# Turning every other slice of the second expert product in place, with GpSimd copying it channels-inside for the way back to the tokens

## The chip, the cores and the metric

The kernel runs on one core of a Trainium2 chip. A core has a matrix engine (TensorE, PE in the profile), three engines for elementwise work (VectorE or DVE, ScalarE or ACT, GpSimd or POOL), and queues that issue DMA transfers (SyncE or SP issues nearly all of them here). The engines run on their own and wait for each other through semaphores. The metric is the device time of one execution in microseconds (us); lower is better.

## The reference

An input of 8192 tokens with 512 channels goes through two layers, each followed by a sum with its own input and a layer norm. The first layer is a long convolution with gates; the change does not touch it. The second layer, cut to what matters:

```
grouped = x.reshape(B, g, t, d)                     # groups of t = 32 tokens
logits  = einsum("bgtd,des->bgtes", grouped, controller) + tie
perm    = logits == max(logits over the experts e)  # 0/1 choice, 32 experts x 4 sets
dispatched   = einsum("bgtd,bgtes->bgesd", grouped, perm)
inner        = relu(einsum("bgesd,desf->bgesf", dispatched, f1) + bias)
intermediate = einsum("bgesf,esfd->bgesd", inner, f2)      # the second expert product
out          = einsum("bgesd,bgtes->bgtd", intermediate, perm)   # back to the tokens
```

Everything is float32.

## The kernel before

`experts` takes the tokens in 4 blocks of 2048 (b.n = 0 to 3), each in two halves of 1024 tokens (u = 0, 1), which are 32 groups of 32 tokens. The 512 channels are taken in four slices of 128 (c = 0 to 3). For each block the steps are:

- `dispatch(b, k)` sums the tokens to the experts on PE (L863) and copies the result from PSUM (L874 on DVE, L876 on ACT).
- `inner(b, k, ...)` multiplies with f1 (PE, L896) and adds into `b.h` on DVE (L902, L910, L912).
- `outer(b, u, c, halves)` is the second expert product for one half and one slice. For each of two halves of the experts it does 64 small matmuls in 32x32 tiles of the array (L933, fed by DMAs of f2 at L925), and two ACT copies (L942) bring the result from PSUM into `stage`. In `stage` a partition is an (expert set, group) pair, and along the partition lie [128 channels][32 experts]. After the second half, two DVE transposes in blocks of 32 x 32 (L946), 64 channels each, bring `stage` to `turned`; now a partition is an (expert set, expert) pair and along it lie [128 channels][32 groups].
- `back(b, u, c, turned)` is the way back to the tokens: for each of the 32 groups one matmul (L962) with the choice `b.permT` as weights (128 x 32) and the 128 channels of that group, `turned[:, :, group]`, as the streamed operand. Four groups go side by side to four column groups of the array. In the profile every f32 matmul is two instructions, so there are 64 per slice. DVE adds the result to `x1` (L969).
- `front(ahead, u)` does the same tokens' first steps for the next block in small pieces that are strewn between the others: A0 to A7 are the output projection of the first layer (`project`: DMA of xt at L750, GpSimd's add of the bias at L772, PE L774, DVE L779), N0 to N3 the norm and its turn (L800, L805, L807), C0 and C1 the choice (L817, L822, L827, L828), T0 and T1 its turn (L836, L837).
- `finish(b, u)` is the last layer norm of a half (L1069 to L1090, with the small chain L721 to L727 and L1077 on DVE and the scaling L1084 on ACT).

`stage` and `turned` are the two halves of one tile:

```
b.big = wk.tile([P, 2, P, T], F32, tag="big", name=f"si_{b.n}_{u}_{c}")
stage, turned = b.big[:, 0], b.big[:, 1]
```

The tag "big" has two buffers, which `dispatch` uses too. PSUM tiles of all these steps come from one pool of four pairs of banks.

The order of PE's work is the order of the program (a manual schedule); for the other engines a scheduler places the instructions. In the loop over slices the way back of a slice is done only after the product of the next slice:

```
outer(b, u, c, [0]); fa(amid)
turned = outer(b, u, c, [1]); fb(behind)
if last: back(*last)
last = (b, u, c, turned)
```

where `fa` and `fb` are pieces of `front` for the next block. The last slice of a block, (u, c) = (1, 3), is sent back between the first two parts and the last two parts of the next block's first `dispatch`. This loop runs for blocks 0, 1 and 2. The last block has an order of its own (`last_block`), with its own product, its transposes in place (L1042) and the same `back_on_pe`.

Of the kernel before, what the change touches and what calls it, by code (L numbers as in the profile page):

```python
# [18 lines left out]
P = 128  # L19
# [4 lines left out]
T = E  # L24
# [655 lines left out]
def experts(tc, i, load, y_dram, out):  # L680
# [10 lines left out]
    nc = tc.nc  # L691
    with (
# [20 lines left out]
        def pair(name):  # L713
            return pp2.tile([P, 1024], F32, tag="pp", name=name)
# [199 lines left out]
        def outer(b, u, c, halves):  # L914


            if halves[0] == 0:
                b.big = wk.tile([P, 2, P, T], F32, tag="big", name=f"si_{b.n}_{u}_{c}")
            stage, turned = b.big[:, 0], b.big[:, 1]
            for half in halves:  # L920
                pss = [pair(f"pi_{b.n}_{u}_{c}_{half}_{rr}") for rr in range(2)]
                for two in range(2):
                    at = 4 * half + 2 * two
                    f2 = wk.tile([P, 2, S, P], F32, tag="f", name=f"f2_{b.n}_{u}_{c}_{at}", bufs=6)
                    nc.sync.dma_start(  # L925
                        out=f2.rearrange("p q s d -> p (q s d)"), in_=i["f2"][c, at // 2]
                    )
                    for q in range(2):
                        for s in range(S):
                            for r in range(R):  # L930
                                rows = slice(r * F, (r + 1) * F)
                                col = r % 2 * 512 + (2 * two + q) * P
                                nc.tensor.matmul(  # L933
                                    pss[r // 2][s * T : (s + 1) * T, col : col + P],
                                    b.h[rows, at + q, s, u * T : (u + 1) * T], f2[rows, q, s, :],
                                    start=True, stop=True,
                                )
                for rr in range(2):
                    o = stage.rearrange("p d (r q) -> p r d q", r=R)[
                        :, 2 * rr : 2 * rr + 2, :, 4 * half : 4 * half + 4  # L940
                    ]
                    nc.scalar.copy(o, pss[rr].rearrange("p (r q d) -> p r d q", r=2, q=4))  # L942
            if 1 in halves:
                for dh in range(2):
                    d = slice(dh * 64, (dh + 1) * 64)
                    nc.vector.transpose(  # L946
                        turned[:, d].rearrange("p d g -> p (d g)"),
                        stage[:, d].rearrange("p d e -> p (d e)"),
                    )
            return turned  # L950

        def back(b, u, c, turned):
# [150 lines left out]
        for n in range(NBLK):  # L1103
            b = Block()
# [4 lines left out]
        b = blocks[0]  # L1109
# [18 lines left out]
        for b in blocks:  # L1128
# [26 lines left out]
            for u in range(2 if ahead else 0):  # L1155
                for c in range(NCT):
                    fa, amid, fb, behind = slots[u * NCT + c]
                    outer(b, u, c, [0])
                    some(ends, 1)
                    fa(amid)  # L1160
                    turned = outer(b, u, c, [1])
                    some(ends, 1)
                    fb(behind)
                    if last:
                        back(*last)
                    if u == 1 and c == 0:
                        ends = finish(b, 0)
                    some(ends, 1)
                    last = (b, u, c, turned)
# [80 lines left out]
```

## Time and profile before

| what | value |
|---|---|
| time, median of 3 runs | 2242.71 us (2237.34 to 2244.29) |
| the profiled execution: its time | 2235.14 us |
| the profiled execution: its span, first to last instruction | 2233.3 us |
| PE clock granted, mean | 0.974 of full |
| the stretch 1576 to 1694 us (loop over slices of block 0): PE busy | 108.2 of 118 us |
| the same stretch: DVE, ACT, POOL busy | 78.0, 47.9, 10.0 us |
| L962, way back of the 24 slices of blocks 0 to 2: PE busy | 90.1 us (1536 instructions) |
| L946, the 48 transposes: DVE busy | 108.1 us |
| L772, GpSimd's adds: POOL busy | 60.6 us (48 instructions) |

The table is read like this: busy times are unions of the engine's instructions, so that matmuls running side by side count once. The loops over slices lie at 1576 to 1694 us (block 0), 1768 to 1890 us (block 1) and 1960 to 2083 us (block 2). In the profile `si` is the tile of `stage` and `turned`, `pc` the PSUM of the way back, `pi` that of the second product, `pd` that of `dispatch`, `xt` the input rows with bias. "PEld" is PE's weight load. A form like "128*32 128x128" names the rows and columns of the array that are used, and the size of the result.

### The profile page before, as it was taken

What the parts mean: (1) busy time and instruction counts of PE and PEld (TensorE: products, weight loads), DVE (VectorE), ACT (ScalarE), POOL (GpSimd) and SP (SyncE); (2) the same over time, 40 slices, a digit from 0 to 9 for tenths busy, and PEclk for the clock granted to TensorE, in tenths of its full rate; (3) what the DMA queues carried; (4) which work ended last, traced back from release to release, by engine and by line L of the source; (5) the groups of instructions that cost most, each with busy time, mean ns of one, the idle gap of its engine ahead of it and who ended that gap; (6) DMA issues with size and microseconds to landing.
All of it is one profiled execution on the core that took longest, in us unless ns stands there. A gap on an engine that the chain in (4) does not pass through costs nothing.

```text
span 2233.3 us, 65558 instructions
## 1 busy us (share of the span) xinstructions
PE 2073.7 (93%) x29472; PEld 1441.0 (65%) x29472; DVE 1380.7 (62%) x1864; ACT 795.7 (36%) x1272; POOL 676.9 (30%) x598
## 2 busy tenths in 40 slices
PE   8999999999998999999999999989999999999874
PEld 3343344444447999999999998555556556556653
DVE  6786776766765553463373373556676667766766
ACT  2444446555552321321221231021243235224424
POOL 3645747766750430250070071211100100110000
PEclk9999999999999999999999999999999999999897
DMA  5312312532434745664573565725763864665474
GB/s 153 105 40 74 104 48 76 198 132 76 145 129 122 220 152 203 194 211 171 161 256 134 180 210 189 241 72 160 235 205 110 270 200 158 207 230 182 135 245 163
DMA packets 187685, 362.60 MB, mean 162 GB/s; under 512 B 77911, under 2 KB 101341, under 8 KB 184333
## 3 DMA queue, kind: packets, MB, share of 16 engines
q1 hardware_dynamic: 181900, 340.05, 46.6%
q10 hardware_dynamic: 5504, 18.35, 2.2%
q8 instruction: 232, 3.80, 0.7%
q14 instruction: 49, 0.39, 0.1%
HBM read 274.47 MB, written 83.89 MB: 160 GB/s over the span
## 4 chain that ended last, share of the span: by engine, by line
PE 73%; DVE 14%; ACT 7%; issue 3%; DMA 2%; POOL 1%; ACTq 0%; DVEq 0%; SPq 0%; POOLq 0%
PE p L329 15%; PE px L588 10%; PE pa L564 10%; PE po L774 10%; PE pz L621 5%; PE py L649 5%; PE pc L962 4%; PE pi L933 3%; PE ph L896 3%; PE pd L863 3%; PE pl L817 2%; ACT o L391 2%; PE pk L286 1%; DVE pf L256 1%; DVE o L407 1%
## 5 line engine op out<-in xcount | busy, mean ns | idle before, releaser
L329 PE MATMUL p<-xs,win 128*128 128x512 f32 x768 | 354.7, 606 | 13.5 <-POOL xs L208 11.2
L329 PEld LDWEIGHTS p<-xs,win 128*128 128x128 f32 x768 | 145.1, 193 | 196.5 <-issue 170.8
L329 PE MATMUL p<-xq,win 128*128 128x512 f32 x576 | 258.7, 597 | 7.4 <-DMA win<-in_W_in 5.3
L610 POOL TENSOR_TENSOR place<-t,hs 128x256 f32<-128x256 f32 x132 | 94.8, 718 | 480.2 <-DVE hs L608 410.2
L774 PE MATMUL po<-wout,yt 128*128 128x512 f32 x512 | 238.1, 611 | 2.3 <-issue 1.9
L564 PE MATMUL pa<-c_in_sb,vk 128*64 128x128 f32 x4096 | 227.3, 274 | 8.1 <-DVE w L414 5.4
L564 PEld LDWEIGHTS pa<-c_in_sb,vk 128*64 128x64 f32 x4096 | 225.7, 138 | 9.9 <-issue 9.5
L588 PE MATMUL px<-place,tab 128*64 128x128 f32 x4096 | 228.1, 273 | 1.7 <-ACT place L571 1.6
L588 PEld LDWEIGHTS px<-place,tab 128*64 128x64 f32 x4096 | 226.1, 136 | 3.1 <-ACT place L571 2.6
L329 PEld LDWEIGHTS p<-xq,win 128*128 128x128 f32 x576 | 109.5, 191 | 147.9 <-issue 134.0
L772 POOL TENSOR_TENSOR xt<-xt,bout 128x512 f32<-128x512 f32 x48 | 60.6, 1285 | 460.3 <-DMA xt<-in_x 385.6
L774 PEld LDWEIGHTS po<-wout,yt 128*128 128x128 f32 x512 | 94.9, 194 | 110.9 <-issue 103.9
L573 DVE COPY place<-pa 128x1024 f32<-128x1024 f32 x64 | 78.3, 1225 | 139.9 <-PE pa L564 136.1
L425 POOL TENSOR_TENSOR w<-o,w 128x512 f32<-128x512 f32 x92 | 114.5, 1274 | 162.6 <-ACT w L397 107.4
L942 ACT COPY si<-pi 128x1024 f32<-128x1024 f32 x96 | 92.9, 1015 | 190.1 <-PE pi L933 156.8
L571 ACT COPY place<-pa 128x1024 f32<-128x1024 f32 x64 | 64.8, 1012 | 254.8 <-PE pa L564 246.8
L407 DVE SCALAR_TENSOR_TENSOR o<-u,chan_sb,o 128x512 f32<-128x512 f32 x192 | 136.4, 746 | 29.4 <-ACT o L391 28.8
L946 DVE STREAM_TRANSPOSE si<-si 128x2048 f32<-128x2048 f32 x48 | 108.1, 2291 | 59.4 <-ACT si L942 59.4
L391 ACT ACTIVATE o<-u,bias,chan_sb 128x512 f32<-128x512 f32 x192 | 141.0, 767 | 0.0
L621 PE MATMUL pz<-c_back_sb,place 64*128 64x128 f32 x2048 | 122.7, 282 | 14.5 <-POOL place L610 14.5
L621 PEld LDWEIGHTS pz<-c_back_sb,place 64*128 64x128 f32 x2048 | 121.9, 198 | 15.4 <-POOL place L610 15.4
L603 ACT COPY hs<-px 128x512 f32<-128x512 f32 x132 | 75.6, 573 | 156.6 <-PE px L588 151.1
(114 smaller groups left out, 3155.5 us busy)
## 6 DMA issues: line engine op xcount, KB each, us to landing
f<-in_f SPq DMA_DIRECT2D x160, 512.0 KB, 5.4
tab<-in_c_mid SPq DMA_DIRECT2D x64, 512.0 KB, 3.8
place<-in_c_out SPq DMA_DIRECT2D x64, 512.0 KB, 4.7
gate<-w SPq DMA_DIRECT2D x32, 512.0 KB, 4.1
x<-w SPq DMA_DIRECT2D x32, 512.0 KB, 3.0
taps<-taps SPq DMA_DIRECT2D x4, 4096.0 KB, 11.1
vk<-taps SPq DMA_DIRECT2D x32, 512.0 KB, 4.0
vk<-gate SPq DMA_DIRECT2D x32, 512.0 KB, 3.7
```

Of the source, the lines that this page charges most:

```text
L329: nc.tensor.matmul(ps, win[self.m][:, slot, self.s, k, :], self.x[tokens][:, k, :], start=(k == 0), stop=(k == 1),)
L391: nc.scalar.activation(pss[n], u[:, t0 + 2 : t0 + 2 + TB], AF.Identity, bias=bias[:, at : at + 1], scale=ch[:, at, 4:5],)
L407: nc.vector.scalar_tensor_tensor(o, u[:, t0 + 1 : t0 + 1 + TB], ch[:, at, 3:4], ps, ALU.mult, ALU.add)
L425: nc.gpsimd.tensor_tensor(wn, o, wn, ALU.add)
L564: nc.tensor.matmul(ps[r * 64 : (r + 1) * 64, c * N1 : (c + 1) * N1], vk[:, half * 8 + c, :], cin[:, r, :], start=True, stop=True,)
L588: nc.tensor.matmul(ps[h * 64 : (h + 1) * 64, j, :, r, :], tab[:, g % 2 * KC + j, r * 64 : (r + 1) * 64], both[:, :, g * KC + j, h * 64 : ( ...
L610: nc.gpsimd.tensor_tensor(o[:, 0], t[:, 0], hs[:, 1], ALU.subtract)
L621: nc.tensor.matmul(ps[:, h, c, :], spec[rows, r, c0 + c, :], cback[rows, r].rearrange("p q n -> p (q n)"), start=(r == 0), stop=(r == 1),)
L649: nc.tensor.matmul(ps[:, q, :], z[:, r * N2 + n0 + q, :], tab[:, q % 4, r, :], start=(r == 0), stop=(r == 1),)
L774: nc.tensor.matmul(ps, got["y"][:, ct, t % 2 * P : (t % 2 + 1) * P], wout[:, ct, :], start=(ct == 0), stop=(ct == NCT - 1),)
L942: nc.scalar.copy(o, pss[rr].rearrange("p (r q d) -> p r d q", r=2, q=4))
L946: nc.vector.transpose(turned[:, d].rearrange("p d g -> p (d g)"), stage[:, d].rearrange("p d e -> p (d e)"),)
```

## The change

For slices with odd c, `turned` gets another layout: along the partition lie [32 groups][128 channels] instead of [128 channels][32 groups], in the same memory. The two DVE transposes of such a slice write back over `stage` instead of into `turned`, and after each of them two GpSimd copies bring its 64 channels to `turned`, 16 groups at a time; they read one element every 32 and write runs of 64 channels. The way back then reads the 128 channels of a group side by side. Slices with even c are as before. It concerns 12 of the 24 slices of blocks 0, 1 and 2; the last block is unchanged.

```diff
@@ outer
             stage, turned = b.big[:, 0], b.big[:, 1]
+            if c % 2:
+                turned = turned.rearrange("p a b -> p (a b)").rearrange("p (g d) -> p d g", d=P)
             for half in halves:
...
             if 1 in halves:
                 for dh in range(2):
                     d = slice(dh * 64, (dh + 1) * 64)
-                    nc.vector.transpose(
-                        turned[:, d].rearrange("p d g -> p (d g)"),
-                        stage[:, d].rearrange("p d e -> p (d e)"),
-                    )
+                    half = stage[:, d].rearrange("p d e -> p (d e)")
+                    if c % 2 == 0:
+                        nc.vector.transpose(turned[:, d].rearrange("p d g -> p (d g)"), half)
+                        continue
+                    nc.vector.transpose(half, half)
+                    for g0 in range(0, T, 16):
+                        nc.gpsimd.tensor_copy(
+                            turned[:, d, g0 : g0 + 16].rearrange("p d g -> p g d"),
+                            stage[:, d, g0 : g0 + 16].rearrange("p d g -> p g d"),
+                        )
             return turned
```

## The prediction

> **What bounds the kernel now.** First the page, its busy times and its chain of work that ended last:
>
> ```profile
> PE 2073.7 (93%) x29472; PEld 1441.0 (65%) x29472; DVE 1380.7 (62%) x1864; ACT 795.7 (36%) x1272; POOL 676.9 (30%) x598
> ...
> PE 73%; DVE 14%; ACT 7%; issue 3%; DMA 2%; POOL 1%; ACTq 0%; DVEq 0%; SPq 0%; POOLq 0%
> ```
>
> PE sets the end. The edit pays where it shortens PE's own work, and costs where PE must wait. It touches `outer`, which runs for 3 blocks x 2 halves x 4 slices = 24 slices; 12 of them have odd c. I write c1, c3 for the odd slices of half 0 and (1,1), (1,3) for those of half 1.
>
> Second, the way back to the tokens (L962) beside two other matmul lines, from the views by source line (ns: min/median/max):
>
> ```profile
> L962 PE MATMUL pc<-si,permT x1536: 377/395/400, 1598.7 to 2079.0; 128*32 128x128 f32 x192
> ...
> L863 PE MATMUL pd<-perm,x x2048: 269/270/578, 1481.0 to 2119.2; 32*128 32x128 f32 x187
> L896 PE MATMUL ph<-dT,f x4096: 216/219/315, 1512.0 to 2138.1; 128*32 128x64 f32 x196
> ```
>
> L863 and L962 both stream 128 columns of f32, but L962 takes 125 ns more. L863 reads its columns side by side; L962 reads `turned[:, :, g]`, a column every 32 elements. L896 has L962's weight shape (128*32), reads 64 columns side by side and shows no such excess: 51 ns under L863 for 64 columns fewer, 0.8 ns a column. So the excess goes with the stride.
>
> Third, the timeline of PE, DVE and POOL around c1 of block 0 and, further down, half 1 (start, duration):
>
> ```profile
> 1596.26 4.51 DVE L946 STREAM_TRANSPOSE si<-si 128x2048 f32<-128x2048 f32 x2 [1.74 <-ACT si L942]
> 1596.91 2.52 POOL L772 TENSOR_TENSOR xt<-xt,bout 128x512 f32<-128x512 f32 x2 [17.32 <-DMA xt<-in_x]
> ...
> 1613.27 3.68 PE L962 MATMUL pc<-si,permT 128*32 128x128 f32 x64
> ...
> 1649.51 2.50 POOL L772 TENSOR_TENSOR xt<-xt,bout 128x512 f32<-128x512 f32 x2 [26.05 <-DMA xt<-in_x]
> 1649.82 0.98 DVE L724 TENSOR_TENSOR rt<-rs 128x4 f32<-128x4 f32 x1
> 1650.84 1.19 DVE L725 TENSOR_TENSOR rt<-rt,ve 128x4 f32<-128x4 f32 x1
> ```
>
> The first pair of transposes is c1's; its way back starts only 12.5 us after they end, because PE does the next slice first. That gap is where the copies must fit. The last three lines show DVE and POOL in each other's way: L724 usually takes 0.16 us and here ends with the first POOL add (1650.76), L725 with the second. The transposes at 1596.26 overlapped POOL adds and kept their 2.25 us each, so transposes are not held.
>
> Fourth, what POOL's instructions cost (groups by shape, POOL alone):
>
> ```profile
> L757 POOL TENSOR_TENSOR xt<-xt,bout 128x1024 f32<-128x1024 f32 x8 | 19.5, 2443 | 96.0 <-DMA xt<-in_x 80.5 <-DMA yt<-y 15.5
> masks.py:199 POOL TENSOR_SCALAR_AFFINE_SELECT ident<-ident 128x128 f32<-128x128 f32 x1 | 0.3, 294 | 0.1
> masks.py:197 POOL MEMSET ident<- 128x128 f32 x1 | 0.2, 205 | 6.7 <-DMA y<-place 6.7
> ```
>
> **The change part by part.**
>
> *Shorter way back on 12 slices.* Now 64 instructions take 3.68 us: 57.5 ns each, and with four column groups side by side 230 ns for 128 columns, 1.80 ns a column. L896, same weight shape and columns side by side, issues 128 in 1.99 us: 15.5 ns, four groups 62 ns for 64 columns, 0.97 ns a column. At that pace the odd slices need 16 x 128 x 0.97 = 1.99 us, so 1.7 us less each: 12 x 1.7 = 20.3 us. Bounds: none if the stride is not the cause; 1.96 us each (23.5 us) if all of the streaming excess (125 of about 233 ns) goes.
>
> *Transposes in place.* 24 DVE instructions change only where they write. L1042 already does the same in place at 2277 ns against L946's 2291: nothing.
>
> *Copies.* 4 per odd slice, 48 in all, 128x1024 f32 each, reading a column every 32 elements and writing runs of 64. No copy by POOL stands in the trace. Low end: MEMSET's slope over the 0.10 us of a one-element memset, 0.105/128 = 0.82 ns an element, so 0.95 us. High end: the two-input add of the same size, 2.44 us, and for the stride that once more by the factor that PE loses to it (1.72 against 0.84 ns a column of streaming, 2.05): 5.0 us. The nearest form is the affine select, one input and one output: (294 - 100)/128 = 1.5 ns an element, 1.65 us a copy. I take 1.65, 6.6 us a slice.
>
> [...]
>
> *Do they fit?* The first copy may start when the first transpose ends, and POOL must have done the xt add queued ahead. From there to L962's start, blocks 0/1/2: c1 13.8/12.2/12.9 us (POOL's L772 of A6 ends last, at 1599.43 in block 0), c3 13.6 in all, (1,1) 10.6/9.9/10.7, (1,3) 7.9/7.1/7.7. At 6.6 us all fit, (1,3) of block 1 with 0.5 us to spare; the limit there is 1.78 us a copy. If that cover is gone, PE waits in order and all later matmuls with it, every microsecond in full.
>
> *What queues behind the copies.* On POOL the order is A6's adds, c1, next block's A0 adds, c3, A2's adds, (1,1), (1,3), A4's adds; in blocks 1 and 2 nearly the same. The adds behind (1,3) wait for their DMA until 1715.74, far after the copies: nothing. The adds ahead of c3 and (1,1) end at 1623.47 and 1652.01, before the copies could start: nothing. The order on PE, DVE, ACT and SP's queue is unchanged, and no DMA is moved.
>
> *DVE held by the copies.* Only instructions like L724 suffer. Around c1 and c3 that is one choice (L828) near the end of the copies: hidden. At (1,1) the copies run 1657.0 to 1663.6 and the small chain L721 to L1077 of `finish` starts at 1663.28: 0.3 us. Also at (1,1), L969 can't end earlier than now (transposes until 1670.68, then L822), which keeps some 0.3 us of the way back's gain. Together 0.6 us a block, 1.8 in all.
>
> Sum: -20.3 + 1.8 = -18.5 us. The profiled execution took 2235.14 us (span 2233.3), the median of the runs is 2242.71, 7.6 above it; the stage is the same in both, so I take the sum off the median: 2224 us.
>
> **The rivals.**
>
> *Copies at the rate of the two-input add, 2.44 us.* 9.8 us a slice: c1 and c3 fit (-1.7 each). At (1,3), gap 7.6 on average, PE waits 2.2 us: +0.5 net. At (1,1) they just fit, but hold DVE's small chain until 1667 or so: L1077 comes 3 us late, the next transposes 1.9 us late, L969 ends near 1674.5 and the matmul that needs its PSUM, at 1674.11 now, comes 0.4 us later than now with the gain gone: +0.4. Per block -2.5, in all -7.5: 2235. For it: stride, and all POOL rows of this size lie at 2.4 us. Against: those read two inputs.
>
> *Slower: the way back waits for GpSimd.* If the stride costs POOL its factor 2.05 on the 1.65 us, a copy takes 3.4 us, a slice 13.6. Late: c1 0.6, (1,1) 3.2, (1,3) 6.0, together 9.8 against a gain of 6.8 a block: +9 in all, 2252; at the ceiling of 5.0 us, late 35.4 a block, +86. It decides from about 3.1 us a copy: two gaps, (4x - 10.4) + (4x - 7.6) = 6.8. For it: the gap of (1,3) is the shortest, and nothing there hides PE. Against: POOL's own rows are far below.
>
> *The change doesn't do what it says for PE.* The 395 ns come from the way four column groups share the array, not from the stride; then the gain is nothing and copies of 1.65 us cost 0 to 2 us: 2243. With 2.44 us it would be +7 from (1,3) alone. Against: L896 has the same groups.
>
> **How the numbers follow.** Forecast 0.49 (-14 to -22 us over 1 to 2 us a copy). Two-input rate 0.22 (0 to -13, half beyond the bound). Late copies 0.18. No gain on PE 0.11 (half within the bound, half slower). A measurement here tells about 0.3%, 6.7 us, from no change. Faster 0.49 + 0.11 = 0.60; same 0.11 + 0.05 + 0.01 = 0.17; slower 0.17 + 0.06 = 0.23. The range goes from the larger saving, with the runs' own spread, 2215, to the first end of the late case, 2253; the forecast's own part of it is 2215 to 2230.
>
> **What would show it.** Right: L962 in two forms, half near 270 ns and 2.0 us a slice; POOL's copies at 1.0 to 1.8 us; no wait of PE on POOL; PE busy 20 us less. Wrong: PE idle before L962 released by POOL, at (1,3) first, then (1,1); L724, L725, L1077 stretched inside the copies; or L962 unchanged at 395 ns. A copy over 3.1 us would by itself make the change a loss.

## The result, and the profile after

The changed kernel takes 2234.34 us (median of 22 runs, 2226.65 to 2241.61) and the kernel before, run beside it, 2238.47 us (22 runs, 2232.96 to 2244.55). The ratio is 0.9975, 95% interval 0.9964 to 0.9986, which at 2238 us is -5.6 us (-8.1 to -3.1). The prediction was -18.5 us: the direction is right, the size is three times too large. The profiled execution took 2228.4 us (span 2226.6, 6.7 less than before; granted clock 0.971).

The page of the profile after, its busy times, chain and copies (group by line: count | busy, mean ns | idle before):

```profile
PE 2058.2 (92%) x29472; PEld 1437.6 (65%) x29472; DVE 1384.0 (62%) x1864; ACT 795.4 (36%) x1272; POOL 771.2 (35%) x646
...
PE 72%; DVE 16%; ACT 7%; issue 3%; DMA 2%; POOL 1%; ACTq 0%; DVEq 0%; POOLq 0%
...
L954 POOL COPY si<-si 128x1024 f32<-128x1024 f32 x48 | 93.3, 1995 | 99.8 <-DVE si L952 99.8
```

The changed line by source line (ns: min/median/max), the copies behind it:

```profile
L970 PE MATMUL pc<-si,permT x1536: 272/338/422, 1600.0 to 2074.3; 128*32 128x128 f32 x192
L954 POOL COPY si<-si x48: 1940/1987/2087, 1599.9 to 2069.8; 128x1024 f32<-128x1024 f32 x48
```

The timeline of block 0, the first odd slice and the copies of (1,1):

```profile
1597.08 2.50 POOL L772 TENSOR_TENSOR xt<-xt,bout 128x512 f32<-128x512 f32 x2 [16.37 <-DMA xt<-in_x]
1599.93 7.77 POOL L954 COPY si<-si 128x1024 f32<-128x1024 f32 x4 [0.35 <-DVE si L952]
...
1614.57 1.95 PE L970 MATMUL pc<-si,permT 128*32 128x128 f32 x64
...
1658.01 7.76 POOL L954 COPY si<-si 128x1024 f32<-128x1024 f32 x4 [2.57 <-DVE si L952]
```

The copies of c1 end at 1607.70, 6.9 us before its way back begins. The matmul of the way back is L970 now (L962 before); half of its instructions stand at 272 ns. A slice with channels inside takes 1.95 us where it took 3.68. Groups by shape, the three loops alone (1570 to 2090 us); in before L962 had 90.1 us there:

```profile
L970 PE MATMUL pc<-si,permT 128*32 128x128 f32 x1536 | 69.7, 335 | 4.2 <-issue 4.2
L721 DVE TENSOR_SCALAR ve<-mv 128x8 f32<-128x8 f32 x5 | 5.3, 1067 | 0.1
```

So the way back lost 20.4 us of PE's time, but PE as a whole lost 15.5 and the span 6.7. The views by line and the page's busy times account for it: -20.4 on the way back, +6.3 on four other matmul lines that run longer over the execution with nothing in them changed (L935 98.9 to 100.7, L863 85.3 to 88.0, L896 68.5 to 69.5, L817 59.3 to 60.1), -1.4 on the rest, and +8.8 of idle time. The rest has one unchanged line that runs shorter, the last block's product (31.8 to 28.5 us), so between two single executions such shifts go both ways.

The idle time, PE's waits in 1570 to 2090 us (us in total, times, longest). Before:

```profile
PE pi L933 <- issue: 11.3, 13, 2.7
PE pi L933 <- ACT si L942: 3.8, 6, 0.8
```

After:

```profile
PE pi L935 <- issue: 14.5, 15, 2.5
PE pi L935 <- ACT si L944: 7.9, 6, 2.1
PE pc L970 <- issue: 4.2, 4, 2.2
PE ph L896 <- issue: 3.6, 2, 2.7
PE pxT L805 <- DVE permT L822: 2.7, 2, 1.6
```

All "issue" waits in this window together rose from 15.8 to 23.0 us, the wait of the second product for ACT by 4.1 us, and a wait of N-turns for L822 is new. The first of these is not like for like: the work stands some 5 us earlier after the change, and the same wait falls behind the window before and into it after:

```profile
2094.56 0.32 PE L896 MATMUL ph<-dT,f 128*32 128x64 f32 x7 [2.92 <-issue]
```

```profile
2089.95 0.49 PE L896 MATMUL ph<-dT,f 128*32 128x64 f32 x13 [2.66 <-issue]
```

Over the same instructions the "issue" waits are 18.7 us before and 23.0 after; the change run again (e15 below) has 20.4. For POOL PE waited only once, 0.36 us at (1,3) of block 0, where the way back took 2.31 us instead of 1.95.

The longer lines come with a lower clock. Windows of the loops (width, busy of PE, PEld, DVE, ACT, POOL; then PEclk), first before, then after:

```profile
1570.00:2090.00 520.00, 488.09 (x11924) 306.61 (x11926) 353.42 (x503) 191.00 (x227) 45.26 (x36) 0.99 0.58 192
```

```profile
1570.00:2090.00 520.00, 475.13 (x12029) 304.36 (x12031) 361.38 (x510) 190.97 (x227) 139.12 (x85) 0.97 0.60 195
...
1714.70:1718.10 3.40, 1.30 (x34) 1.03 (x32) 3.30 (x8) 1.97 (x2) 2.45 (x2) 1.00 0.64 259
1718.20:1724.90 6.70, 6.02 (x66) 4.63 (x67) 3.37 (x3) 2.02 (x2) 0.00 (x0) 0.50 0.01 2
1725.00:1728.00 3.00, 3.00 (x31) 1.28 (x32) 0.22 (x1) 0.00 (x0) 0.00 (x0) 1.00 0.00 0
```

PE worked 1.30 of 3.4 us, and the next 6.7 us ran at half clock. From 1570 us to the half-clock window behind the wait at L896 shown above (it ends at 2098.4 us before and at 2093.6 after), the trace has 17.1 us at half clock before (4 stretches) and 34.1 us after (8 stretches). The next stretch, 10.2 us, stands in both, at 2101.8 us before and at 2097.0 after.

### The profile page after: what moved, and what is told of

Same layout as the page of the kernel before. It is cut to its first block, busy times and chain, and to the rows that moved or that the text cites. A ratio compares the mean times of both kernels' runs of the same rounds, so it can differ in the third digit from the quotient of the medians.

```text
span 2226.6 us, 65625 instructions
## 1 busy us (share of the span) xinstructions
PE 2058.2 (92%) x29472; PEld 1437.6 (65%) x29472; DVE 1384.0 (62%) x1864; ACT 795.4 (36%) x1272; POOL 771.2 (35%) x646
## 4 chain that ended last, share of the span: by engine, by line
PE 72%; DVE 16%; ACT 7%; issue 3%; DMA 2%; POOL 1%; ACTq 0%; DVEq 0%; POOLq 0%
PE p L329 15%; PE px L588 10%; PE pa L564 10%; PE po L774 9%; PE pz L621 6%; PE py L649 5%; PE pi L935 3%; PE ph L896 3%; PE pd L863 3%; PE pc L970 3%; PE pl L817 2%; ACT o L391 2%; PE pk L286 2%; DVE pf L256 1%; DVE o L407 1%
## 5 line engine op out<-in xcount | busy, mean ns | idle before, releaser
L944 ACT COPY si<-pi 128x1024 f32<-128x1024 f32 x96 | 93.0, 1014 | 180.5 <-PE pi L935 161.7
L621 PE MATMUL pz<-c_back_sb,place 64*128 64x128 f32 x2048 | 123.2, 283 | 14.5 <-POOL place L610 14.5
L954 POOL COPY si<-si 128x1024 f32<-128x1024 f32 x48 | 93.3, 1995 | 99.8 <-DVE si L952 99.8
```

Source lines behind the costliest of these rows:

```text
L621: nc.tensor.matmul(ps[:, h, c, :], spec[rows, r, c0 + c, :], cback[rows, r].rearrange("p q n -> p (q n)"), start=(r == 0), stop=(r == 1),)
L954: nc.gpsimd.tensor_copy(turned[:, d, g0 : g0 + 16].rearrange("p d g -> p g d"), stage[:, d, g0 : g0 + 16].rearrange("p d g -> p g d"),)
```

## The experiments

Ratios are to the kernel before, run beside it on the same chip; "us" is (ratio - 1) x 2238. Diffs are against the changed kernel.

| run | edit | ratio (95%) | us |
|---|---|---|---|
| the change | | 0.9975 (0.9964 to 0.9986) | -5.6 |
| e15_again | the change again | 0.9969 (0.9948 to 0.9990) | -6.9 |
| e1_nocopy | no copies | 0.9938 (0.9918 to 0.9959) | -13.9 |
| e2_copyonly | copies, way back as before | 0.9991 (0.9974 to 1.0009) | -2.0 |
| e3_direct | DVE writes the layout itself | 1.0074 (1.0053 to 1.0096) | +16.6 |
| e4_direct_all | the same, 24 slices | 1.0167 (1.0142 to 1.0192) | +37.4 |
| e5_shift | 64 more PE instructions ahead | 0.9968 (0.9948 to 0.9987) | -7.2 |
| e6_no11 | no copies at (1,1) | 0.9976 (0.9961 to 0.9991) | -5.4 |
| e7_small | copies in quarters | 0.9997 (0.9979 to 1.0015) | -0.7 |
| e8_later | last norm a slice later | 0.9977 (0.9960 to 0.9995) | -5.1 |
| e9_no_half1 | no copies in half 1 | 0.9949 (0.9929 to 0.9969) | -11.4 |
| e10_no_half0 | no copies in half 0 | 0.9949 (0.9925 to 0.9972) | -11.4 |
| e11_swap | odd slices of half 0, even of half 1 | 0.9993 (0.9976 to 1.0010) | -1.6 |
| e12_nocopy_all | no copies, 24 slices | 0.9894 (0.9869 to 0.9919) | -23.7 |
| e13_unawaited | copies that nobody awaits | 0.9955 (0.9937 to 0.9973) | -10.1 |
| e14_pick | c1, c3, (1,2), (1,3) | 0.9990 (0.9972 to 1.0008) | -2.2 |
| e16_cover | A7 moved over the wait | 0.9991 (0.9973 to 1.0009) | -2.0 |
| e17_cover_before | the same in before | 1.0009 (0.9995 to 1.0023) | +2.0 |
| e18_cover_nocopy | the same without copies | 0.9960 (0.9941 to 0.9980) | -9.0 |

**The two sides of the change alone.**

```diff
                     nc.vector.transpose(half, half)
-                    for g0 in range(0, T, 16):
-                        nc.gpsimd.tensor_copy(...)
+            if c % 2:
+                return stage.rearrange("p a b -> p (a b)").rearrange("p (g d) -> p d g", d=P)
             return turned
```

> The odd slices are transposed in place and the way back reads that same half of the tile as if the channels lay inside; the 48 copies by GpSimd are left out, so the odd slices carry wrong elements. PE keeps its shorter way back (1.95 us instead of 3.68), GpSimd does nothing there. Theory A (PE's saving of 20.4 us is paid out only in part, because other chains follow close behind: PE's own code supply, the gaps with releaser 'issue', and the DVE and ACT chain at the start of half 1): still only -7 to -12 us against the kernel before, because taking the copies away gives back at most the DVE instruction L721 that waits for GpSimd (1.5 us a block) and 0.4 us at (1,3). Theory B (the copies cost the missing 13 us, by holding DVE or by being late): -18 to -21 us.

```diff
-            return turned
+            return stage if c % 2 else turned
```

> The odd slices are transposed in place and GpSimd makes its 48 copies, but nobody reads them: the way back reads the transposed half with its stride, as before. The result is the reference's. Theory A: +0 to +4 us against the kernel before (the hold on DVE's L721 at (1,1), nothing else). Theory B: +10 to +14 us.

Measured: -13.9 us without copies (-18.4 to -9.2), -2.0 us with copies alone (-5.8 to +2.0). The first lies between the ranges of the two theories; the second is below both, with 0 inside its interval. So the copies cost nothing that shows beside the old way back, a faster way back without copies brings two thirds of its 20.4 us, and with both only a third is left. Something of PE's saving is lost even with no copy in the program. In the profile of e1 PE's idle time over the execution is 167.5 us (span less busy) against 159.6 before, and three waits of the second product show where it goes:

```profile
PE pi L935 <- issue: 15.6, 16, 3.7
PE pi L935 <- ACT si L944: 7.9, 6, 2.1
PE pi L935 <- DVE x L974: 3.7, 3, 1.7
```

Before, the same three are 11.3, 3.8 and 0.9 us.

**The layout without GpSimd.**

```diff
-                    nc.vector.transpose(half, half)
-                    for g0 in range(0, T, 16):
-                        nc.gpsimd.tensor_copy(...)
+                    nc.vector.transpose(turned[:, d], stage[:, d])
```

> The odd slices' transposes write the layout with the channels inside themselves (output pattern of 64 channels x 32 groups, a step of 128 between groups), no copies and no GpSimd. If a strided write costs DVE nothing (2.29 us stays), this is e1 with right results: theory A -7 to -12 us, theory B -18 to -21 us. If DVE pays for the stride as PE does for its read (double, 4.6 us a transpose, 55 us more DVE in the three blocks), PE waits for DVE at half 1 and the time is that of before or above, 0 to +15 us.

> As e3, for all 24 slices: PE has about 41 us less to do than before. Theory A: the gains stay partial, since the even slices' savings run into the same chains (code supply above all, which PE now outruns twice as often): -10 to -20 us against the kernel before. Theory B: -36 to -41 us, if transposes stay at 2.29 us. If they double, slower than before by 10 to 50 us.

 (the same edit for every c)

Both lose, by 16.6 and 37.4 us. Groups of e3 in 1570 to 2090 us, and two of its waits of PE there:

```profile
L952 DVE STREAM_TRANSPOSE si<-si 128x2048 f32<-128x2048 f32 x22 | 84.0, 3893 | 27.2 <-ACT si L944 27.2
L950 DVE STREAM_TRANSPOSE si<-si 128x2048 f32<-128x2048 f32 x24 | 54.1, 2291 | 34.2 <-ACT si L944 34.2
```

```profile
PE pi L935 <- DVE x L972: 11.1, 3, 3.9
PE pp L836 <- DVE x L972: 10.0, 3, 3.3
```

A transpose that writes with the step takes 3893 ns instead of 2291, and PE waits for DVE's add behind it. GpSimd was the cheaper place for the step here (-5.6 us with its copies, +16.6 us with DVE's step).

**Where PE waits with no releaser.** Counted over PE's records (weight loads, matmuls and its semaphore steps), the waits with no releaser between 1570 and 2090 us stand at one place of a group of 256: 18 of over 0.15 us (15.7 us) before, 22 (23.0 us) after. The page has the instruction queue (packets, MB, share of the DMA engines):

```profile
q8 instruction: 232, 3.80, 0.7%
```

That is 16.4 KB a packet, and 59389 records of PE over 256 make 232. The second product is 128 weight loads and 128 matmuls in 1.9 us, a whole group; where PE waited, the next group came 3.4 to 5.5 us after PE had entered the one before (8 in 10 of these 40 waits). In the kernel before, of the groups with at least 4.5 us of PE's work none of 60 ended in a wait, of those under it 18 of 34. e5 moves the code by 64 instructions, with 32 more turns in block 0:

```diff
-                    for k in range(NCT):
+                    for k in range(NCT * (5 if b.n == 0 and u == 0 and m == 0 else 1)):
+                        k = k % NCT
```

> The changed kernel with the 8 turns of the first norm (block 0, half 0, N0) done five times over: 32 turns more, 64 more PE instructions (weight load and matmul), same result, some 4 us more PE work at that place. Everything after it is the same code, 64 instructions later in PE's code. Theory A1 (PE's idle gaps that the trace calls 'issue' are PE waiting for its next 256 instructions, one of the 232 packets of 16 KB of queue q8): every such gap falls 32 weight load + matmul pairs earlier in the work. The gap of the changed kernel in the product after c1's way back, after 100 of 128 matmuls, stands after about 68; the one that is always there in c1's product after 126 stands after about 94; the sum of the gaps in the three blocks may change by some us either way, so the time is +0 to +8 us against the changed kernel (-6 to +3 against before). Theory A2 (the gaps are a wait for f2's data or for PSUM): they stay after 100 and 126 matmuls.

The product at 1591 us in block 0, after the change and in e5:

```profile
1591.71 1.89 PE L935 MATMUL pi<-f,h 32*32 32x128 f32 x126
1596.08 0.40 PE L935 MATMUL pi<-f,h 32*32 32x128 f32 x2 [2.48 <-issue]
```

```profile
1591.62 1.47 PE L936 MATMUL pi<-f,h 32*32 32x128 f32 x94 [0.61 <-DVE x L779]
1593.41 0.69 PE L936 MATMUL pi<-f,h 32*32 32x128 f32 x34 [0.32 <-issue]
...
1675.47 0.69 PE L936 MATMUL pi<-f,h 32*32 32x128 f32 x18 [3.09 <-issue]
```

The gap moved from after 126 matmuls to after 94, the 32 that went in: these waits are for code. c1's way back is 1.73 us shorter in both, but only in e5 does the stretch from c1's to c2's way back fall by as much (13.07 before, 12.43 after, 11.35 in e5, mean of the blocks); in the changed kernel code gaps eat most of the rest (0.33 and 0.83 us in block 0, 1.26 in block 1, 0.23 in block 2). e5 pays elsewhere (3.09 us at 1675), and its time is that of the change.

**The start of half 1.** c3's way back comes earlier, but DVE does not. PE's wait before, and the timeline after:

```profile
1649.71 0.88 PE L933 MATMUL pi<-f,h 32*32 32x128 f32 x42 [0.76 <-ACT si L942]
```

```profile
1641.55 4.50 DVE L950 STREAM_TRANSPOSE si<-si 128x2048 f32<-128x2048 f32 x2 [1.62 <-ACT si L944]
1643.14 1.95 PE L970 MATMUL pc<-si,permT 128*32 128x128 f32 x64
1646.55 1.21 DVE L977 TENSOR_TENSOR x<-pc,x 128x1024 f32<-128x1024 f32 x1
1649.08 0.15 DVE L721 TENSOR_SCALAR ve<-mv 128x4 f32<-128x4 f32 x1
1649.27 0.20 ACT L722 ACTIVATE rt<-ve 128x4 f32<-128x4 f32 x1 [7.75 <-DVE ve L721]
1649.38 1.91 ACT L944 COPY si<-pi 128x1024 f32<-128x1024 f32 x2
1650.42 1.87 PE L935 MATMUL pi<-f,h 32*32 32x128 f32 x124 [2.13 <-ACT si L944]
```

DVE is at the next slice's transposes until 1646.05; its row leads to L721, ACT's L722 stands 7.75 us for it with L944 behind, and PE waits 2.13 us (0.76 before). What that wait costs depends on the clock behind it. The stretch from c3's to (1,0)'s way back, with the same wait in it, took 9.66 us in each of the three passes at full clock (one in the profile of the change, one in e15, one in e5), and 10.67 to 10.92 us in the four passes of the change and of e15 that hold 3.3 to 3.4 us at half clock. So one window at half clock costs 1.0 to 1.3 us here, and with it c3's saving is gone (10.71 us before, mean of the blocks). Two experiments work on this place:

```diff
-                    if u == 1 and c == 0:
+                    if u == 1 and c == 1:
                         ends = finish(b, 0)
...
+                some(ends, 99)
                 dT = dispatch(ahead, 0, [0])
```

> The changed kernel with the last norm of half 0 (finish) begun one slice later, behind the way back of (1,0) instead of that of c3, its rest drained before the next dispatch; result right. Theory A (c3's saving of 1.7 us is lost because DVE's row L779, L977, L786, then finish's L1077 and L1078, then L721 comes no earlier, and ACT and PE wait for it: 'pi <- ACT si' 2.1 us a block): with finish's statistics out of that row, that wait falls below 1 us, and the stretch from c3's way back to that of (1,0) falls from 10.4 us on average to 8.5 to 9.5; in all -8 to -12 us against before, unless the norm, now closer to the end of the block, makes PE wait there. Rival: DVE is bound by the transposes alone there; the wait stays at 2 us and the time is that of the changed kernel, -3 to -8.

PE's wait for L944 falls from 7.9 to 5.9 us and c3's stretch by 1 us, but (1,3) now waits for POOL (2.5 us in 3 times) and DVE: -5.1 us, no different from the change.

```diff
-                (f0, "T0 C1", f1, "A7"), (f1, "N0", f0, "T1"),
+                (f0, "T0 C1", nothing, ""), (f1, "A7 N0", f0, "T1"),
```

> The change, with the piece A7 (8 matmuls, 3.7 us of PE) done in slice (1,1) ahead of N0, after c3's way back, not in slice (1,0) before it. In the change PE stands 2.13 us there in each block, waiting for ACT's L944, which stands behind L722 and so behind DVE's row. Theory (c3's saving is lost in that wait, and each wait of this length that falls into one window of 3.41 us also brings PE 3.41 us at half clock behind it): the wait is covered by A7, PE idle falls by some 6 us in the three blocks, at least one or two of the slow windows go, and the time is 6 to 9 us under that of the change: some -11 to -15 us against before. Rival (the wait belongs to DVE's row and only moves, as with the last norm begun one slice later): L721 needs A7's sum, so the row comes about 1 us later and the gain is lost at (1,1) or (1,3): -5 us against before, no difference from the change.

> The same move of A7 in the kernel before. PE waits only 0.76 us at that place there, and those waits are followed by no slow window in the profile. Theory: -2 us, at most 0.8 us a block. Rival (A7 simply stands better there, whatever the way back costs): as much as the change gains from it, -6 us or more.

> The same move of A7 in the kernel without copies (odd slices read the block transposed in place as if the channels were inside, so other elements; GpSimd's copies are left out). Theory: the wait of 2.1 us a block is covered here too: 6 to 9 us under the kernel without copies, some -20 to -23 us against before, so that nearly all of the 20 us of PE's saving comes through once waits and copies are out of the way. Rival: no difference from the kernel without copies, -14 us.

The expected gain did not come: -2.0, +2.0 and -9.0 us, each 2 to 5 us worse than its kernel without the move, though no single one of these three differences is clear of the intervals. Waits of e16 in 1570 to 2090 us, and one of its gaps in the timeline:

```profile
PE pi L935 <- issue: 30.8, 18, 4.2
PE pi L935 <- ACT si L944: 1.5, 3, 0.5
```

```profile
1654.98 1.70 PE L935 MATMUL pi<-f,h 32*32 32x128 f32 x104
1660.60 0.71 PE L935 MATMUL pi<-f,h 32*32 32x128 f32 x24 [3.91 <-issue]
```

The wait for ACT went from 7.9 to 1.5 us as meant, and the wait for code from 14.5 to 30.8. A reading that fits: a wait that PE spends for ACT is time in which its code arrives; taken away, the next two products stand close together and wait for code instead. It is not separated from a second effect of the move: A7, 3.7 us of work in 8 matmuls, no longer stands between two products ahead of the covered wait, and a code gap of 1.36 us opens there (1643.41 us in block 0). In e17 the same happens on a smaller scale: the second product waits 1.5 us for ACT (3.8 before) and 16.5 us for code (11.3 before).

**The copies beside the faster way back.** Three kernels leave them out in part, one makes them without awaiting them, one cuts them smaller:

```diff
-                    for g0 in range(0, T, 16):
+                    for g0 in range(0, 0 if (u, c) == (1, 1) else T, 16):
...
+            if (u, c) == (1, 1):
+                return stage.rearrange("p a b -> p (a b)").rearrange("p (g d) -> p d g", d=P)
```

> The changed kernel without GpSimd's four copies of slice (1,1) (12 fewer in all); its way back reads the half transposed in place as in the run without copies, so this slice carries wrong elements. The other 36 copies stay. Theory C1 (what the copies cost, some 8 us, is at (1,1): they hold DVE's L721 for 1.5 us, and the PSUM that L822 frees then comes late for PE): -11 to -15 us against the kernel before, as without any copies. Theory C2 (they cost through lateness at (1,3), or spread over all four places): -5 to -9 us.

e9 and e10 do the same with `c % 2 and u == 1` and `c % 2 and u == 0`:

> The changed kernel without GpSimd's copies in half 1 (slices (1,1) and (1,3) carry wrong elements, read as in the run without copies); c1 and c3 keep theirs. Theory D1 (the copies cost their some 8 us in half 1, where either place holds PE: DVE's L721 at (1,1), and at (1,3) the copies themselves, which end 7.8 us after the first transpose when PE, freed at (1,1), is there sooner): -11 to -15 us against the kernel before, as without any copies. Theory D2 (the cost is in half 0, or is no cost at all but scatter of the code gaps): -4 to -8 us.

> The counterpart: no copies in half 0 (c1 and c3 carry wrong elements), (1,1) and (1,3) keep theirs. D1: the changed kernel's time, -3 to -8 us against the kernel before. D2: -11 to -15 us.

e13 keeps every copy, and odd slices return that view of `stage`:

> The changed kernel with all 48 copies, which nobody reads: the way back of the odd slices reads the half transposed in place with its channels inside, as in the run without copies (so these slices carry wrong elements). PE waits for DVE, never for GpSimd; DVE is held by the copies as in the changed kernel (L721 some 1.1 us on average). If the copies cost by holding DVE: the changed kernel's time, -4 to -8 us against the kernel before. If they cost by being waited for: the time without copies, -11 to -16 us.

```diff
-                    for g0 in range(0, T, 16):
+                    for g0 in range(0, T, 4):
```

> The changed kernel with the copies cut in four: 4 groups of 64 channels each, 192 copies of 256 elements instead of 48 of 1024; result right. If a copy is 0.1 us and 1.85 ns an element, 0.57 us each and 9.2 us a slice instead of 7.8. Theory C1 (hold on DVE): L721 waits at most 0.6 us instead of 1.5, but more DVE instructions fall into the longer row of copies, and (1,3) is late by 1.5 us more: -5 to -10 us against before. Theory C2 (lateness): -1 to -5 us.

 (each slice `g0 : g0 + 16` becomes `g0 : g0 + 4`)

In the changed kernel the copies hold DVE's small L721 of the last norm. Its five instances take 1067 ns on average against 169 before; the three that stand inside copies, one a block, take 1.64 to 1.68 us. Through them L822 and PE's turn of N2 come late:

```profile
1664.15 1.64 DVE L721 TENSOR_SCALAR ve<-mv 128x8 f32<-128x8 f32 x1
1673.02 1.09 PE L805 MATMUL pxT<-ident,x 128*128 128x128 f32 x8 [1.57 <-DVE permT L822]
```

e6 frees L721 (168 ns) and takes 1.1 us of waits for POOL at (1,3) in exchange: -5.4 us, nothing gained. e7 has the hold at its worst (groups, then the wait of PE behind it):

```profile
L954 POOL COPY si<-si 128x256 f32<-128x256 f32 x192 | 110.4, 650 | 99.4 <-DVE si L952 99.4
...
L721 DVE TENSOR_SCALAR ve<-mv 128x8 f32<-128x8 f32 x5 | 9.7, 1936 | 0.1
```

```profile
PE pxT L805 <- DVE permT L822: 9.2, 3, 3.2
```

Smaller copies did not let DVE in sooner: L721 takes 1936 ns on average, 1067 in the change. e9 and e10 come out the same, -11.4 us, so the runs do not put the cost in one half: of the two theories, e9 fits the one and e10 the other. e13 lies between e1 and the change. The intervals of all three overlap with those of e1 and of the change, so how the cost is shared stays open.

**Other slices, and all of them.** e11 takes `c % 2 != u`, e14 the four slices named in the table, e12 all slices without copies:

> The changed kernel with the other two slices in half 1: c1 and c3 in half 0, (1,0) and (1,2) in half 1; result right. From the trace of before, the first transpose of (1,0) and of (1,2) ends some 10 us before the way back, that of (1,3) only 7.6 us; and no L721 of the last norm lies in the copies of (1,2). D1: the copies are covered in half 1 too, so -7 to -12 us against the kernel before; (1,0) gains little, because DVE's transposes of (1,1) hold PE next. D2: as the changed kernel, -3 to -8 us.

> Another choice of slices: c1, c3, (1,2) and (1,3) instead of c1, c3, (1,1) and (1,3); result right. In the traces so far the stretch behind (1,2) keeps all of its 1.7 us (PE's own work follows there), and without copies at (1,1) L721 of the last norm is not held. If the place decides what a slice pays: -9 to -13 us against the kernel before. If the sum of copies decides: the changed kernel's time, -4 to -8 us.

> As the run without copies, for all 24 slices of the three blocks (all of them carry wrong elements): PE has 41 us less to do, DVE and ACT the same as before, GpSimd nothing. Theory A (PE's saving meets its code supply and the DVE and ACT chain): -18 to -28 us against the kernel before, with more PE idle time by releaser 'issue' (21.5 us in the run with the odd slices alone) and by ACT and DVE. If PE were the only bound: -36 to -41 us.

Neither choice of other slices paid: -1.6 and -2.2 us, less than either theory had for them. e12 saves 40.8 us on the way back (90.1 to 49.3 us) and 23.7 of it comes through, 58% against 68% in e1: in microseconds the loss without copies grows with the saving, from 6.5 to 17.1 us. That the share falls is not clear of the intervals.

> The changed kernel itself, on the chip of the other two and against the same runs of the kernel before, as their yardstick: -3 to -8 us, as in its 22 runs (-5.6).

The change came out as before, -6.9 us (-11.6 to -2.2).

**The clock over all runs.** The mean granted clock of the kernel before is 0.9737 over its 29 runs beside e15; e15's is 0.9708, and the first runs of the change have 0.9700. e1 has 0.9724 and e2 0.9739, on a chip where the kernel before has 0.9730. Over all runs of all kernels, each counted once and taken within its kernel, 0.001 of clock goes with some 1.4 us of time. By that the lower clock goes with some 4 us of e15 (2.8 x 1.4). In the traces the clock changes on a fixed grid of 3.41 us (in the profile before, half clock begins at 1722.92, 1777.53 and 1914.06 us, 16 and 40 steps apart), and a window at half clock goes with a low busy share of PE in the window before. Over all 20 profiles, 1570 to 2100 us:

| PE busy in a window | windows | next one at half clock |
|---|---|---|
| under 0.4 | 80 | 80 |
| 0.4 to 0.5 | 63 | 48 |
| 0.5 to 0.6 | 98 | 39 |
| 0.6 to 0.9 | 611 | 60 |
| 0.9 and more | 2237 | 12 |

Nearly all of the 72 in the last two rows follow a window that was itself at half clock. Of the 2626 windows at full clock with PE busy for 0.6 or more, one was followed by half clock. This is read off the traces; no run set the clock by itself. That the lower clock costs some 4 us is a correlation and not an experiment, and a wait of PE lengthens the run and, by the table, goes with half clock behind it, so the slope can hold some of the wait's own time.

## Why the prediction was right in direction and wrong in size

**Shorter way back.** Right in size: 20.3 us forecast, 20.4 measured; the 272 ns were forecast as 270 and the 1.95 us a slice as 2.0. The stride is the cause, and the rival "no gain on PE" is out.

**Passed on in full.** This is the step that failed. The sum let all of it but 1.8 us reach the end, because PE "sets the end" by the page. It does so as the last of a row of waiters, not as an engine that is never late: 31 us of its 520 were idle already, half of them for its own code. e1 puts a number on it: with no copies at all, -13.9 of -20.4. Its profile shows three waits of PE in the place of the saving: 4.3 us more for code, 4.1 us more for ACT behind DVE's row, 2.8 us more for DVE's add, with some other waits shorter (7.9 us of idle time in all). Named places are the code gaps (c1, shown by e5) and DVE's row at the start of half 1 (c3), where the half clock behind the wait takes what is left. In e16 the wait for ACT was covered and the wait for code grew by more, which fits one budget of idle time but does not prove it. The busy time of an engine was taken for work that can be shortened freely, and its unnamed "issue" share of 3% was read past.

**Copies.** Mis-sized: 1.995 us each, not 1.65; inside the bounds and under the 2.44 us of the first rival, but over the 1.8 us that was to show the forecast right. They fit their gaps, and "late copies" is out: PE waited for POOL 0.36 us at most. At (1,3) that was in part luck. The copies take 7.75 us there, more than the forecast's limit for block 1, and PE came to this way back later after the first transpose than before (8.1 us against 7.1); they ended 0.3 us behind its start in block 0 and 0.3 and 0.8 us ahead of it in blocks 1 and 2. In e8 PE waited 2.5 us for them.

**DVE held by the copies.** Forecast at 0.3 us for the chain at (1,1) and as much for L969; the chain's L721 alone was held 1.5 us in each block, and its follower L822 made PE wait 2.7 us in all (0 before). The term was mis-sized, but to free L721 (e6) gave back no time that shows.

**Copies at no other cost.** Wrong. Two pairs differ only in the copies: the change and e1 (-5.6 and -13.9), e16 and e18 (-2.0 and -9.0), so they cost 7 to 8 us beside the faster way back, with 5 to 6 us of uncertainty either way, and nothing that shows beside the old one (e2). The intervals of the first pair lie apart, though that of e15 overlaps with e1's (0.9948 to 0.9959); those of the second, which ran on one chip, overlap a little too (0.9973 to 0.9980). In both pairs the clock is lower with copies (0.9700 against 0.9724, 0.9692 against 0.9719), which by the slope of 1.4 us goes with 3 to 4 us of it. Through which waits it comes was not settled: e6, e7, e9, e10 and e13 each touch a part, and none takes it all.

The first rival's total, -7.5 us, lies near the result by luck. No copy took 2.44 us, PE stood for them at (1,3) once for 0.36 us and not 2.2 us a block, and the hold of DVE's chain at (1,1), which did come, left most of the gain there: the stretch from (1,1)'s to (1,2)'s way back fell from 10.78 to 9.48 us (mean of the blocks).

## What to carry to other kernels

The busy time that an edit takes off the busiest engine is an upper bound; before passing it on, go to the stage and list that engine's waits, those with no releaser too, and ask for each whether the shorter work leaves it more to wait for. For dense small matmuls count instructions: a group of 256 that PE works off in less than some 4.5 us here ended in a wait for code in half of the cases (18 of 34 before). Price the second half of an edit beside the first and not alone: copies whose cost did not show in e2 cost some 7 to 8 us where the engine they serve had become faster.

## What the runs showed of the hardware

- PE's code, as these traces show it: queue q8 has 232 packets of 16.4 KB, one for each 256 of PE's 59389 records, and all waits with no releaser over 0.15 us between 1570 and 2090 us (18 before, 22 after) stand at one place of a group of 256. Where PE had to wait, the next group came 3.4 to 5.5 us after it had entered the last (8 in 10 of 40 waits). PE stood for it 18.7 us before, 23.0 after and 35.5 in e16, over the same instructions of some 520 us.
- Over the 20 profiles (1570 to 2100 us) a window of 3.41 us in which PE was busy under 0.4 was followed by half clock 80 times of 80; 55 of these windows touched no single gap of PE as long as 3.41 us.
- With four column groups, the f32 operand of the way back streams at 1.80 ns a column when it is read at a step of 128 bytes (before), side by side at 0.95 (after): 3.68 and 1.95 us for 16 x 128 columns.
- A DVE transpose of 128x2048 f32 that writes at a step takes 3.89 us against 2.29 (e3).
- A GpSimd copy of 128x1024 f32 that reads at a step takes 2.0 us (after), one of 128x256 0.65 us (e7).
